# Layer 0 of a four-layer network: the first stage of the state-space scan moved up, its output products put at one tile

## The chip, the cores and the metric

The kernel runs on one core of a Trainium2 chip. A core has a matrix engine (PE, with its weight loads listed as PEld), a vector engine (DVE), an activation engine (ACT), a general engine (POOL) and a sequencer that only issues transfers here (SP); each takes its own instructions in program order and waits for the others through semaphores. The metric is device time in microseconds (us), the median of the runs; a profile is taken of one execution of its own.

## The reference, cut to what matters

The network has four layers on an image batch of 4 x 96 x 64 x 64. Only layer 0 is touched. It is two Mamba blocks (`NLAYERS` = 2) over sequences of 4096 positions, followed by a small fusion and a batch norm:

```
h  = layernorm(seq);  xs, z = split(h @ in_w)
xc = silu(sum_k conv_w[:, k] * shift(xs, k) + conv_b)
dt, Bm, Cm = split(xc @ xproj_w)
delta = softplus(dt @ dt_w + dt_b)
state[t] = exp(delta * A) * state[t-1] + delta * Bm * xc     # 192 channels x 16 states
y = sum over states(state * Cm) + Dp * xc
seq = seq + (y * silu(z)) @ out_w
```

Layers 1 to 3 (a convolution block, attention and feed-forward, a Fourier block) follow after it.

## The kernel before, in words

**Items and tiles.** The sequence is cut into 4 pieces of 1024 positions. With 4 batches and 2 blocks this gives 32 *items* (`items`; index k; the block i alternates every four items). An item's 192 x 16 recurrences are 24 *tiles* of 128 lanes x 1024 positions, in the list `order`. Each tile is one DVE scan (`scan`, L595). Four of them per third use a product `u` that DVE makes first (L586), two take it from POOL (`up`, L571, group GP), two straight from PE (`uta`, group GA). The decay `da`/`dap` is one exponential on ACT (`exp`, L560). After a pair of tiles POOL multiplies the states by C (`times_c`, L600) and PE sums them over the states into a bank y (`sum_y`, L617). `start_y` (L610) puts Dp * xc into that bank first, and `gate` (L628) multiplies y by silu(z). State tiles `hs` are four buffers, given out by `keeps`: a scan that takes one anew has to wait for the `sum_y` of the group that had it before.

**One program order, written by hand.** The loop near the end of `layer0` runs over m, one step per tile, and writes for each step what every engine issues: the scan, the fill of a PE bank for a coming tile (`fills`), the exponential three tiles ahead (one ahead for GP), `times_b`, `times_c`, then `start_y`, `sum_y`, `gate` by the tables `starts`, `sums`, `gates` (tile number counted from the item's own first tile, so 29 is tile 5 of the next item), the output product `project` and `project_z` with `finish` (L647 to L661), and last the steps of the *first stage* of coming items. PE, DVE, ACT and POOL keep this order exactly (`manual_schedule`). SP isn't in that list: the framework places its transfers itself.

**The first stage.** `first_stage(k)` makes all that item k needs before its scans: normalization, convolution `xc` in three parts (PE L232, copied by ACT L356), silu (L367), the product with `xproj` (L246), its copy `dbl` (L386), `delta` in three parts, softplus (L394), a write of delta to memory (`dd`), the product `du` = delta * xc on POOL (L424) and its write (`ud`, both L413), z, and a transposed, weighted copy `uta` (turned by PE L433, taken back by ACT L438 *into delta's own buffer*, weighted by `weigh`, L451). `at_slot(t)` puts a step at step m = 24k - 24 + t: slots 0 to 23 run beside the scans of item k-1, negative ones beside item k-2, slots from 24 beside item k itself. Below, "tile t" is the tile of the running item at which a step stands: slot -2 is tile 22, slot 27 is tile 3.

**Buffers that matter.** PE's results of the first stage and of the output go through two PSUM tiles in turn (`tile_ps`). `x` has two buffers: one is loaded for the normalization of the next-but-one item (slot -20), one for the residual at the output (`load_x`, L275, at 29 in the main loop). `delta` has one buffer.

Of the kernel before, what the change touches and what calls it, by code (L numbers as in the profile page):

```python
# [50 lines left out]
class Net:  # L51
# [43 lines left out]
    def layer0(self, dram, scratch):  # L95
        tc, nc, ins = self.tc, self.nc, self.ins
        x_in = ins["x"]
        with ExitStack() as ctx:
# [23 lines left out]
            w_x = cp.tile([C + 1, 2, 4, DIN], F32, name="w_x")  # L122
# [3 lines left out]
            dtw = cp.tile([97 + DTR, 2, DIN], F32, name="dtw")  # L126
# [9 lines left out]
            n = cp.tile([C + 1, T + 3], F32, name="n")  # L136
# [11 lines left out]
            GP, GA = 2, 3  # L148
# [78 lines left out]
            def spread(ws, rhs, p):  # L227

                ps = tile_ps(128)
                for k, (w, shift) in enumerate(ws):  # L230
                    for at, rows in both:
                        nc.tensor.matmul(  # L232
                            ps[rows],
                            w[:, 64 * p : 64 * p + 64],
                            rhs[:, at.start + shift : at.stop + shift],
                            start=k == 0,
                            stop=k == len(ws) - 1,
                            skip_group_check=True,
                        )
                return ps  # L240
# [37 lines left out]
            def first_stage(k):  # L278

                b, s, i = items[k]  # L280
                m = made[k]
                steps = {}

                def at_slot(t):
                    def keep(f):
                        steps.setdefault(t - 24, []).append(f)

                    return keep
# [61 lines left out]
                def parts_of(name, ws, rhs, slots, bufs):  # L350


                    def into(p, ps):
                        if p == 0:
                            m[name] = early.tile([128, 3, MB], F32, name=name, tag=name, bufs=bufs)
                        nc.scalar.copy(m[name][:, p], ps)  # L356

                    for p, (t, out) in enumerate(slots):
                        at_slot(t)(lambda p=p: m.update({(name, p): spread(ws, rhs, p)}))
                        at_slot(out)(lambda p=p: into(p, m[name, p]))  # L360


                parts_of("xc", [(w_x[:, i, k], k) for k in range(4)], n, ((-6, -4), (-3, -2), (0, 0)), 2)

                @at_slot(1)
                def _():
                    nc.scalar.activation(m["xc"], m["xc"], AF.Silu)  # L367
                    if k:
                        silu_z(k - 1)
                    exp_set()  # L370
# [4 lines left out]
                nb = 6 * NST + DTR  # L375
                dbl = m["dbl"] = dbls[k % 2]

                @at_slot(3)
                def _():
                    m["ps"] = [tile_ps(128), tile_ps(128)]  # L380
                    join([ps[:nb] for ps in m["ps"]], xproj[:, :, i], m["xc"])

                @at_slot(4)
                def _():
                    for at, ps in zip(halves, m["ps"]):
                        nc.scalar.copy(dbl[:nb, at], ps[:nb])  # L386
                    cd = m["cd"] = dram.tile([2 * NST, T], F32, name="cd", tag="cd", bufs=2)
                    nc.sync.dma_start(cd, dbl[: 2 * NST])

                parts_of("delta", [(dtw[:, i], 0)], dbl, ((5, 5), (6, 6), (7, 7)), 1)  # L390

                @at_slot(7)
                def _():
                    nc.scalar.activation(m["delta"], m["delta"], AF.Softplus)  # L394
                    exp_set()

                @at_slot(8)
                def _():
                    m["tb"] = y_bank(3 * k - 2)[:, : 8 * 2 * NST].rearrange("p (q s) -> p q s", q=8)
                    for q in range(8):  # L400
                        nc.tensor.transpose(
                            m["tb"][:, q], dbl[: 2 * NST, q * 128 : q * 128 + 128], self.ident[: 2 * NST, : 2 * NST]
                        )

                @at_slot(9)
                def _():
                    m["bt"] = cp.tile([128, 8, 4], F32, name="bt", tag="bt", bufs=2)
                    nc.scalar.copy(m["bt"], m["tb"][:, :, 4 * GA : 4 * GA + 4])
# [3 lines left out]
                    for at, rows in both:  # L412
                        nc.sync.dma_start(to.rearrange("(p c) t -> c p t", p=3)[:, :, at], m[name][rows])  # L413

                @at_slot(8)
                def _():
                    spread_out("delta", "dd")

                @at_slot(10)
                def _():  # L420
                    m["du"] = m["delta"]
                    if k == 0:
                        m["du"] = early.tile([128, 3, MB], F32, name="z", tag="z", bufs=2)
                    (nc.gpsimd if k else nc.vector).tensor_mul(m["du"], m["delta"], m["xc"])  # L424
                    spread_out("du", "ud")
# [29 lines left out]
                        )  # L455

                e = 0
                for t, count in ((19, 4), (20, 5), (21, 5), (22, 4), (23, 6), (24, 6), (28, 2)):
                    at_slot(t)(lambda of=range(e, e + count): weigh(of))
                    e += count  # L460

# [44 lines left out]
            items = [(b, s, i) for s in range(NSC) for i in range(2) for b in range(B)]  # L506
# [14 lines left out]
            keeps = {(0, 0): 0, (0, GP): 1, (0, 1): 2, (0, GA): 3, (1, 0): 0, (1, GP): 1, (1, GA): 2, (1, 1): 3}  # L521
            keeps |= {(2, GA): 0, (2, 0): 3, (2, GP): 1, (2, 1): 2}
            ends = {max(t for t, x in enumerate(order) if x[:2] == (p, g)): (p, g) for p in range(3) for g in range(4)}
            sums = {4: (0, 0), 8: (0, 1), 9: (0, GP), 11: (0, GA), 13: (1, 0), 17: (1, 1), 18: (1, GP), 19: (1, GA)}
            sums |= {21: (2, GA), 22: (2, 0), 25: (2, 1), 27: (2, GP)}
            starts = {4: 0, 12: 1, 18: 2}
            gates = {13: 0, 21: 1, 29: 2}
            NTL = len(order)
            last = len(items) * NTL
# [100 lines left out]
            def project(k):  # L630
                b, s, i = items[k]
                pss = made[k]["out"] = [tile_ps(), tile_ps()]
                for at, ps in zip(halves, pss):
                    w = fus[:, 0] if i else self.ident[:C, :C]
                    nc.tensor.matmul(ps, w, made[k]["x"][:, at], start=True, stop=False)

            def project_z(k):
                b, s, i = items[k]
                join(made[k]["out"], fo if i else out_w, made[k]["z"], start=False)
# [35 lines left out]
            with tc.manual_schedule(engines=engines):  # L675
                gp = global_pool()
                first = min(stages[0])
                for m in range(first, last + 19):
                    k, t = divmod(m, NTL)
                    if 0 <= m < last:  # L680
                        scan(m)
                    if m == -12:
                        fill(0)
                    if t in fills and 0 < 24 * k + fills[t] < last and m >= 0:
                        fill(24 * k + fills[t])
                    if 0 <= m + 1 < last and on_pool(m + 1):
                        exp(m + 1)
                    if 0 <= m + AHEAD < last and not on_pool(m + AHEAD):
                        exp(m + AHEAD)
                    if t in b_slots:  # L690
                        ahead, p, j = b_slots[t]
                        if 0 <= k + ahead < len(items):
                            times_b(k + ahead, p, j)
                    for back, f in ((1, times_c), (3, keep_state)):
                        k0, t0 = divmod(m - back, NTL)
                        if 0 <= k0 < len(items) and t0 in ends:
                            f(k0, *ends[t0])
                    for k0 in range(max(k - 1, 0), min(k + 1, len(items))):
                        at = m - NTL * k0
                        if at in starts:  # L700
                            start_y(k0, starts[at])
                        if at in sums:
                            sum_y(k0, *sums[at])
                        if at in gates:
                            gate(k0, gates[at])
                        if at == 29:
                            made[k0]["x"] = load_x(*items[k0])
                        if at == 32:
                            project(k0)
                        if at == 33:  # L710
                            project_z(k0)
                        if at == 34:
                            finish(k0)
                    for k0 in range(max(k - 1, 0), min(k + 3, len(items))):
                        for f in stages[k0].get(m - NTL * k0, ()):
                            f()
                    if m in (10, 11):
                        next(gp)
# [877 lines left out]
```

## Time and profile before

| | |
|---|---|
| median of 3 runs | 3871.77 us (3863.05 to 3873.45) |
| the profiled execution | 3861.26 us, its span 3859.4 us |
| first scan starts | 69.1 us |
| last scan of layer 0 ends | 2553.2 us |
| busy from 100 to 2500 us: DVE | 2191.23 us of 2400 |
| the same: POOL | 2077.30 us |
| the same: PE | 1980.54 us, mean granted clock 0.89 |
| the same: ACT | 1904.46 us |
| a DVE scan (L595, with state and rep) | 2337 ns |
| a POOL product with C (L600) | 4180 ns |
| an ACT exponential (L560) | 1149 ns |

A busy time is the sum over an engine's instructions. A wait is named by the engine that waits and by what released it. Layer 0 takes the span's first two thirds; an item takes 71.8 to 85.2 us from its first scan to the next item's, the very first one 87.9.

### The profile page before, as it was taken

What the parts mean: (1) busy time and instruction counts of PE and PEld (TensorE: products, weight loads), DVE (VectorE), ACT (ScalarE), POOL (GpSimd) and SP (SyncE); (2) the same over time, 40 slices, a digit from 0 to 9 for tenths busy, and PEclk for the clock granted to TensorE, in tenths of its full rate; (3) what the DMA queues carried; (4) which work ended last, traced back from release to release, by engine and by line L of the source; (5) the groups of instructions that cost most, each with busy time, mean ns of one, the idle gap of its engine ahead of it and who ended that gap; (6) DMA issues with size and microseconds to landing.
All of it is one profiled execution on the core that took longest, in us unless ns stands there. A gap on an engine that the chain in (4) does not pass through costs nothing. (4 is left out here: it accounts for less than half of the span.)

```text
span 3859.4 us, 46789 instructions
## 1 busy us (share of the span) xinstructions
PE 3226.2 (84%) x15326; PEld 1468.0 (38%) x15326; DVE 2989.2 (77%) x2644; ACT 2722.0 (71%) x5456; POOL 2566.3 (66%) x922
## 2 busy tenths in 40 slices
PE   7788888888888888888788888756899998999988
PEld 3232333323332333232322232226544534666643
DVE  5898888899989898998899999962473384444649
ACT  6787877888778787887788787741245686656557
POOL 1898888888888888988888998941001064534527
PEclk8898888899888898998898998757899999999999
DMA  7566555566656565665655766546200000011101
GB/s 189 146 152 163 144 150 148 148 157 160 160 142 157 137 156 145 166 153 143 155 150 145 170 156 167 142 121 209 98 1 1 1 1 6 17 34 34 39 9 58
DMA packets 171643, 446.62 MB, mean 116 GB/s; under 512 B 48756, under 2 KB 50750, under 8 KB 168064
## 3 DMA queue, kind: packets, MB, share of 16 engines
q1 hardware_dynamic: 171400, 443.64, 44.7%
q8 instruction: 121, 1.98, 0.2%
q14 instruction: 122, 1.00, 0.1%
HBM read 369.97 MB, written 73.50 MB: 115 GB/s over the span
## 5 line engine op out<-in xcount | busy, mean ns | idle before, releaser
L600 POOL TENSOR_TENSOR hs<-hs,crep 128x2048 f32<-128x2048 f32 x384 | 1597.3, 4180 | 333.2 <-DVE hs L595 248.2
L560 ACT ACTIVATE da<-ddb,nega 128x1024 f32<-128x1024 f32 x576 | 661.3, 1149 | 157.4 <-DVE hs L595 138.3
L595 DVE TENSOR_TENSOR_SCAN hs<-da,state,rep 128x1024 f32<-128x1024 f32 x288 | 667.9, 2337 | 46.8 <-PE rep L544 35.2
L571 POOL TENSOR_TENSOR up<-udb,brep 128x1024 f32<-128x1024 f32 x192 | 452.7, 2358 | 74.9 <-DMA udb<-ud 60.5
L617 PE MATMUL y<-hs,sel_r 128*32 128x512 f32 x3072 | 441.9, 650 | 25.5 <-POOL hs L600 25.5
L232 PE MATMUL ps<-n,w_x 97*64 97x512 f32 x1536 | 425.9, 699 | 0.0
L549 PE MATMUL rep<-dbl,sel_b 32*128 32x512 f32 x768 | 250.7, 730 | 175.7 <-DVE hs L595 174.6
L451 ACT ACTIVATE uta<-delta,bt 128x192 f32<-128x192 f32 x1024 | 375.3, 442 | 0.0
L595 DVE TENSOR_TENSOR_SCAN hs<-dap,state,up 128x1024 f32<-128x1024 f32 x144 | 336.3, 2335 | 39.4 <-PE y L617 16.9
L595 DVE TENSOR_TENSOR_SCAN hs<-da,state,u 128x1024 f32<-128x1024 f32 x144 | 338.1, 2348 | 21.7 <-PE y L617 6.8
L544 PE MATMUL rep<-ident,uta 128*128 128x128 f32 x1536 | 224.4, 293 | 74.4 <-DVE hs L595 73.8
L586 DVE TENSOR_TENSOR u<-udb,rep 128x1024 f32<-128x1024 f32 x192 | 236.0, 1229 | 64.1 <-PE rep L549 26.3
L560 ACT ACTIVATE dap<-ddb,nega 128x1024 f32<-128x1024 f32 x192 | 213.9, 1114 | 86.7 <-DVE hs L595 86.1
L544 PEld LDWEIGHTS rep<-ident,uta 128*128 128x128 f32 x1536 | 182.1, 150 | 169.0 <-DVE hs L595 89.2
L232 PEld LDWEIGHTS ps<-n,w_x 97*64 97x64 f32 x1536 | 133.8, 158 | 289.7 <-issue 251.2
L1154 POOL CAST hq<-y 128x1536 fp8e5<-128x1536 f16 x64 | 93.9, 1466 | 217.6 <-issue 122.6
L595 DVE TENSOR_TENSOR_SCAN hs<-da,rep 128x1024 f32<-128x1024 f32 x96 | 216.9, 2277 | 20.1 <-PE rep L544 16.7
L586 DVE TENSOR_TENSOR rep<-udb,rep 128x1024 f32<-128x1024 f32 x192 | 232.3, 1210 | 0.0
L617 PEld LDWEIGHTS y<-hs,sel_r 128*32 128x32 f32 x3072 | 62.3, 111 | 360.9 <-issue 233.9
L549 PEld LDWEIGHTS rep<-dbl,sel_b 32*128 32x128 f32 x768 | 65.1, 201 | 301.8 <-issue 164.1
L246 PE MATMUL ps<-xc,xproj 64*102 64x512 f32 x384 | 129.3, 824 | 58.0 <-ACT xc L367 58.0
L1293 POOL TENSOR_TENSOR av<-av,ec 128x780 f32<-128x780 f32 x32 | 58.7, 1836 | 133.5 <-ACT av L1290 133.5
(275 smaller groups left out, 6290.9 us busy)
## 6 DMA issues: line engine op xcount, KB each, us to landing
ddb<-dd SPq DMA_DIRECT2D x768, 128.0 KB
udb<-ud SPq DMA_DIRECT2D x768, 128.0 KB
crep<-cd SPq DMA_DIRECT2D x512, 128.0 KB
dd<-delta SPq DMA_DIRECT2D x64, 384.0 KB
band<-in_band SPq DMA_DIRECT2D x24, 1024.0 KB
ud<-delta SPq DMA_DIRECT2D x62, 384.0 KB
brep<-cd SPq DMA_DIRECT2D x128, 128.0 KB
x<-in_x SPq DMA_DIRECT2D x32, 384.0 KB
```

The source lines that it names most:

```text
L232: nc.tensor.matmul(ps[rows], w[:, 64 * p : 64 * p + 64], rhs[:, at.start + shift : at.stop + shift], start=k == 0, stop=k == len(ws) - 1, ...
L246: nc.tensor.matmul(ps, w[rows, p], x[rows, p], start=start and p == 0, stop=p == 2)
L451: nc.scalar.mul(m["uta"][:, q, :, 32 * s4 : 32 * s4 + 32].rearrange("t (p j) d -> t p j d", p=3), m["udt"][:, :, q].rearrange("t p (j d) - ...
L544: nc.tensor.transpose(x[:, q * 128 : q * 128 + 128], made[k]["uta"][:, q, 2 * h + j], self.ident)
L549: nc.tensor.matmul(x[:, at], sel_b[rows, g], made[k]["dbl"][rows, at], start=True, stop=True)
L560: nc.scalar.activation(da, made[k]["dd", h, j], AF.Exp, scale=nega[:, col : col + 1])
L571: nc.gpsimd.tensor_mul(up, made[k]["ud", p][:, j], made[k]["brep", GP])
L586: nc.vector.tensor_mul(u, made[k]["ud", h][:, j], x)
L595: nc.vector.tensor_tensor_scan(hs[:, 1:], made[k].pop(("da", t)), u, st, ALU.mult, ALU.add)
L600: nc.gpsimd.tensor_mul(hs[:, :, :T], hs[:, :, 1:], twice(made[k]["crep", g]))
L617: nc.tensor.matmul(made[k]["y", p][row : row + 32], sel_r, made[k]["hs", p, g][:, j, at], start=False, stop=True, skip_group_check=True,)
L1154: nc.gpsimd.tensor_copy(q, y2, saturate=False)
```

## The change: what it does

It leaves every operation as it is and moves steps in the hand-written order.

- Convolution: part 3 goes from slot 0 to slots -2 (PE) and -1 (copy). Silu, with silu of the previous item's z and the reload of the exponential table, goes from slot 1 to -1.
- `xproj` from 3 to 1, the copy `dbl` from 4 to 2; delta's parts from 5, 6, 7 to 3, 3, 5 (PE) and 5, 5, 6 (copy); softplus from 7 to 6.
- The transposed B from 8 and 9 to 6 and 7, the write of delta from 8 to 7, `du` and its write from 10 to 8.
- `weigh`: twelve of its 32 instructions go from tiles 23 and 0 (six each) to tiles 0, 1, 2, 3 (three each).
- Sums into y: (0,1) from 8 to 7, (1,0) from 13 to 14, (2,1) from 25 to 26. The term Dp * xc of the first third from tile 4 to tile 0.
- Output: the residual's load from 29 to 27; `project` stays at 32 (tile 8), `project_z` joins it there from 33, `finish` goes from 34 to 33. These three now stand in a loop of their own after the sums and gates.

```diff
-                parts_of("xc", [(w_x[:, i, k], k) for k in range(4)], n, ((-6, -4), (-3, -2), (0, 0)), 2)
-                @at_slot(1)
+                parts_of("xc", [(w_x[:, i, k], k) for k in range(4)], n, ((-6, -4), (-3, -2), (-2, -1)), 2)
+                @at_slot(-1)
                 def _():
                     nc.scalar.activation(m["xc"], m["xc"], AF.Silu)
...
-                @at_slot(3)
+                @at_slot(1)
                     join([ps[:nb] for ps in m["ps"]], xproj[:, :, i], m["xc"])
-                @at_slot(4)
+                @at_slot(2)
                         nc.scalar.copy(dbl[:nb, at], ps[:nb])
-                parts_of("delta", [(dtw[:, i], 0)], dbl, ((5, 5), (6, 6), (7, 7)), 1)
-                @at_slot(7)
+                parts_of("delta", [(dtw[:, i], 0)], dbl, ((3, 5), (3, 5), (5, 6)), 1)
+                @at_slot(6)
                     nc.scalar.activation(m["delta"], m["delta"], AF.Softplus)
-                @at_slot(8)
+                @at_slot(6)
                     m["tb"] = y_bank(3 * k - 2)[:, : 8 * 2 * NST].rearrange("p (q s) -> p q s", q=8)
-                @at_slot(9)
+                @at_slot(7)
                     m["bt"] = cp.tile([128, 8, 4], F32, name="bt", tag="bt", bufs=2)
-                @at_slot(8)
+                @at_slot(7)
                     spread_out("delta", "dd")
-                @at_slot(10)
+                @at_slot(8)
                     m["du"] = m["delta"]
...
-                for t, count in ((19, 4), (20, 5), (21, 5), (22, 4), (23, 6), (24, 6), (28, 2)):
+                for t, count in ((19, 4), (20, 5), (21, 5), (22, 4), (24, 3), (25, 3), (26, 3), (27, 3), (28, 2)):
...
-            sums = {4: (0, 0), 8: (0, 1), 9: (0, GP), 11: (0, GA), 13: (1, 0), 17: (1, 1), 18: (1, GP), 19: (1, GA)}
-            sums |= {21: (2, GA), 22: (2, 0), 25: (2, 1), 27: (2, GP)}
-            starts = {4: 0, 12: 1, 18: 2}
+            sums = {4: (0, 0), 7: (0, 1), 9: (0, GP), 11: (0, GA), 14: (1, 0), 17: (1, 1), 18: (1, GP), 19: (1, GA)}
+            sums |= {21: (2, GA), 22: (2, 0), 26: (2, 1), 27: (2, GP)}
+            starts = {0: 0, 12: 1, 18: 2}
...
-                        if at == 29:
+                    for k0 in range(max(k - 1, 0), min(k + 1, len(items))):
+                        at = m - NTL * k0
+                        if at == 27:
                             made[k0]["x"] = load_x(*items[k0])
                         if at == 32:
                             project(k0)
+                            project_z(k0)
                         if at == 33:
-                            project_z(k0)
-                        if at == 34:
                             finish(k0)
```

## The prediction

> **What bounds the kernel now.** I read first how busy the engines are in layer 0, then who DVE waits for, then the places in time where those waits stand. Busy times of three items, 1, 8 and 12 (columns: stretch, its length, then busy us of PE, PEld, DVE, ACT, POOL, granted PE clock, DMA share, GB/s):
>
> ```profile
> 157.00:228.80 71.80, 59.27 (x320) 22.64 (x318) 69.61 (x39) 61.24 (x123) 67.15 (x20) 0.98 0.57 144
> 703.60:782.80 79.20, 62.86 (x320) 23.53 (x318) 71.17 (x40) 63.23 (x129) 67.24 (x20) 0.91 0.58 148
> 1004.80:1084.30 79.50, 67.45 (x320) 24.85 (x318) 71.20 (x40) 61.59 (x123) 67.16 (x20) 0.86 0.61 149
> ```
>
> DVE has some 70 to 71 us of work in every item; the items differ in what it waits. Item 1 shows that 71.8 us can be had, 8 and 12 lose about 8 each. So the floor is DVE's work, and a reordering can win DVE's waits and nothing else. From 160 to 2550 us DVE waits for (us in total, times, longest):
>
> ```profile
> DVE hs L595 <- PE rep L544: 46.1, 14, 4.7
> DVE hs L595 <- PE y L617: 28.2, 26, 4.9
> DVE hs L595 <- ACT x L647: 26.2, 4, 6.9
> DVE u L586 <- PE rep L549: 22.3, 18, 2.1
> DVE u L586 <- DMA udb<-ud: 9.7, 6, 1.9
> DVE hs L595 <- ACT dap L560: 9.7, 19, 1.4
> DVE hs L595 <- ACT shift L655: 6.5, 1, 6.5
> ```
>
> These are 148.7 us. In time they fall into two places. *Tiles 17 to 21 of 13 items*: the rows L544, L586 <- L549 and udb, 46.1 + 22.3 + 9.7 = 78.1, and about ten of the 28.2 (0.8 a time at tile 18): 88 us. *Tile 10*: ACT x and shift, 32.7, and the rest of L617, 18: 51 us, of which items 3, 4, 5, 12, 18 and 21 have 5 to 7 each. L560 is tile 2.
>
> The first place, item 8, in order of time (start, duration, instruction; brackets: idle before and releaser), SP, then POOL, ACT, DVE:
>
> ```profile
> 737.65 0.31 SPq L661 DMA_DIRECT2D scratch<-x  x1
> 746.41 0.33 SPq L275 DMA_DIRECT2D x<-in_x  x1
> 746.84 1.24 SPq L413 DMA_DIRECT2D ud<-delta  x2
> ```
> ```profile
> 738.28 3.45 POOL L424 TENSOR_TENSOR delta<-delta,xc 128x1536 f32<-128x1536 f32 x1
> ```
> ```profile
> 752.99 0.58 ACT L438 COPY delta<-y 128x512 f32<-128x512 f32 x1 [5.75 <-DMA ud<-delta]
> ```
> ```profile
> 756.56 2.35 DVE L595 TENSOR_TENSOR_SCAN hs<-da,state,rep 128x1024 f32<-128x1024 f32 x1 [3.23 <-PE rep L544]
> 760.74 1.23 DVE L586 TENSOR_TENSOR u<-udb,rep 128x1024 f32<-128x1024 f32 x1 [1.84 <-DMA udb<-ud]
> ```
>
> POOL has du at 741.73. Its write stands on SP behind a load of x, which itself stands behind the write of the output and waits until PE has read the x buffer (L299, tile 13): it leaves at 746.84, five us late. ACT may not overwrite delta before the write has read it, so L438 holds ACT for 5.75 us, behind it PE's turns and fills, and tile 17 comes late. The waits of SP count this (same columns as above):
>
> ```profile
> SPq L275 <- PE ps L299: 116.8, 13, 10.9
> ```
>
> Thirteen times, in the 13 items.
>
> The second place, item 12, on PE and then DVE:
>
> ```profile
> 1029.56 3.70 PE L635 MATMUL ps<-x,ident 96*96 96x512 f32 x4 [1.43 <-DMA x<-in_x]
> 1033.19 1.94 PE L617 MATMUL y<-hs,sel_r 128*32 128x512 f32 x8
> 1036.05 4.51 PE L246 MATMUL ps<-z,out_w 64*96 64x512 f32 x12
> 1040.48 1.06 PE L617 MATMUL y<-hs,sel_r 128*32 128x512 f32 x8
> ```
> ```profile
> 1041.72 2.35 DVE L595 TENSOR_TENSOR_SCAN hs<-dap,state,up 128x1024 f32<-128x1024 f32 x1 [6.16 <-ACT x L647]
> ```
>
> The products wait 1.43 us for x, then run at half clock (in item 9 the same three groups take 1.96, 1.06 and 2.82), and behind them stands the sum (0,GP) whose state buffer scan 10 needs. L647 is only the last ACT instruction before: the sum, ending at 1041.54, is what released it.
>
> [...] part 2 of the convolution, behind steady work, takes 3.65 us, part 3, behind an idle 2.85 us and a fill, 5.84 (item 12). But 1.43 us of idle time was enough at 1029.56[...]
>
> **The change part by part.**
>
> *SP's order and du (tile 8).* In the changed program both loads of x follow `cd` directly, with PE's reads of them an item old, and `ud` follows one `ddb` load; the output's write comes after `ud`. POOL's du goes ahead of one `up` (2.35) and one product with C (4.18): in item 12 it would start where the group (0,GA) ends, 1033.9, instead of 1040.3, 6.4 us earlier. Softplus's end (1031.5 there) allows it. SP is then free, so `ud` leaves 9 to 11 us earlier in the 13 items, lands with the measured 6.2 us (746.84 to 752.99) well before tile 14, and L438 doesn't wait. What du delays on POOL, `up` of (1,1) and the product (1,0) by 3.45 us, is wanted at tiles 14 and 16; at 1044 it has caught up. Sum (1,0) at tile 14 for 13 fits. Removed: 88, of which I take 80 as small waits stay.
>
> *Output at tile 8.* x is loaded after `dbl`, which is some 5 us earlier (below), so the 1.43 us go. `project` and `project_z` together, 1.96 + 2.82, now follow sum (0,1); a delta part (1.08) and the transposes of B (0.68) leave the row. From the fill of tile 8 to the end of sum (0,GP) PE needs 1.13 + 1.06 + 1.96 + 2.82 + 1.06 = 8.0 us, against 9.4 in item 9 (803.96 to 813.33), at full clock. DVE needs two scans and two products from there, and has them: tile 10 falls to some 0.3 us a time, 51 to 10. Removed: 40.
>
> *Silu at tile 23.* This is what costs. PE puts part 3 straight behind the last sum of tile 22 (ends 1077.98 before item 13), 3.65 at full clock: 1081.6. On ACT follow the copy, 0.56, table, silu, silu, table (1.28 + 1.48 + 1.47 + 1.28 = 5.5, as in the trace at 1091.49 to 1096.94), an exponential (1.05 to the next start), three `weigh` (0.35 each): 1089.8. `dap` then lets scan 2 go 1.2 later, 1091.0, where without a wait it would go at 1090.2. So 0.8 us at tile 2, 1.3 in items whose sum ends 0.4 later, in place of 0.3 on average (9.7 / 30): + 0.7 x 30 = 20. The fill of tile 0, now behind part 3, ends at 1082.8 and is wanted at 1083.0: no cost at full clock, and if late it takes the place of the tile 2 wait. Twelve `weigh` (4.2 us) in tiles 0 to 3 fill what silu left there; the last ones at tile 4 end as before, within 0.3 us. `xproj` can start when silu ends (1084.9), and with two exponentials and six `weigh` between, `dbl` is copied at about 1094.5, not 1101.
>
> *Rest.* Dp * xc at tile 0 needs a bank whose gate was tile 21: nothing. Sums (0,1), (2,1): POOL's products end 1025.6 and at 1085, one tile ahead: nothing. delta's parts, tables, counts of instructions and bytes: the same. `finish` one tile earlier: about -2 at the end.
>
> *PE's pauses.* New ones: before the fill of tile 3 (about 2 us), before delta (2), before the first uta fill (2.4). A half-clocked fill, delta part, fill (1.1 each) before scan 7 would cost about 1 us, and some in tile 8. From below nothing; from above 2 us an item. I take 0.4 x 31 = 12.
>
> Sum: -80 - 40 + 20 + 12 - 2 = -90, 3861.3 to 3771. The profiled execution is 10.5 us under the median of the three; I put the median between the two, 3780.
>
> **The rivals.**
> - *Only the queue is mended.* The tile-10 wait stays, since the pauses leave PE at half clock in front of two products: -80 + 20 + 12 - 2, about 3811, up to 3840 with twice the tile 2 cost. For: 5 to 7 us came from a pause of only 1.43. Against: x isn't late any more.
> - *No change* (3860 to 3883): both gains real, and 3 us an item lost again (92 / 31), where ACT's row at tile 23 is held by a late part 3. Against: PE ran part 2, just ahead, at 3.65 us, without a pause between.
> - *Slower.* PE is at half clock from tile 5 to 10 in every item, not in six. The pass from the fill of tile 8 to the sum took 15.6 us in item 12 for 9.4 in item 9: 6.2 x 31 = 192 on top of the sum, 3780 + 192 = 3970. It decides from 3.3 us an item on (103 us from 3780 to 3883, over 31 items). For: three pauses of 2 us ahead of that stretch. [...]
>
> **How the numbers follow.** A median of three spread by 0.3% (3863 to 3873) tells no less than that: 12 us. Both waits gone 0.62 (own range 3745 to 3815), only the queue 0.18, no change 0.06, slower 0.14. Faster 0.62 + 0.18 = 0.80. The range leaves out slower and no change, 0.20: upper end 3860. Lower end: 88 and 51 all gone and no new cost at tile 2 or by pauses, 3861 - 141 = 3720, which I think hardly possible as tile 2's chain is serial; 3740.
>
> **What would show it.** No row of SP's x load waiting for L299 and no L438 wait on `ud` above 2 us; DVE waits for L544 under 10 us in all. At tile 2 a wait of 0.8 to 1.3 us for `dap` in nearly every item: if it is 3 or more, part 3 ran at half clock. At tile 10 no wait over 2 us. POOL's du before the `up` of tile 9. Items of 73 to 75 us each. Wrong I am if waits at tiles 7, 8 or 10 return in most items, or if POOL, at 67 of 73 us, becomes what DVE waits for.

## The result, and the profile after

The changed kernel takes **3873.12 us** (median of 20 runs, 3866.59 to 3899.71), the kernel before 3867.98 (20 runs beside them, 3845.14 to 3886.94): a ratio of **1.0028**, 95% interval 1.0010 to 1.0047. That is no change, or slower by less than half a percent; it lies in the range that the prediction called no change (3860 to 3883), and 93 us above the forecast 3780. The profiled execution of after has a span of 3885.5 us, 26 more than before's 3859.4. That is more than the 5 us between the medians, because the profiled execution of after is 14 us above its median and that of before 7 below.

The table is DVE's idle time in layer 0 between one scan and the next, by tile, worked out from the traces (us per item, mean of 32 items; the sum is over all tiles of layer 0). DVE idles 0.1 to 0.3 us at some tiles in every kernel, as at tile 12 before; tiles that never have more are left out.

| kernel | tile 2 | 7 | 10 | 12 | 15 | 16 | 17 | 18 | 21 | sum |
|---|---|---|---|---|---|---|---|---|---|---|
| before | 0.52 | 0.00 | 1.66 | 0.27 | 0.08 | 0.00 | 1.54 | 1.14 | 0.59 | 219 |
| after | 1.30 | 0.25 | 0.50 | 0.54 | 0.28 | 0.64 | 0.00 | 1.73 | 1.15 | 244 |

The wait at tile 17 is gone, that at tile 10 mostly; tiles 2, 7, 12, 15, 16, 18 and 21 have taken more than both gave. Items 5 and 12 of after (stretch, length, busy us of PE, PEld, DVE, ACT, POOL, granted PE clock, DMA share, GB/s):

```profile
469.98:548.42 78.44, 64.80 (x318) 23.45 (x318) 69.84 (x40) 63.40 (x131) 67.11 (x20) 0.89 0.60 151
1019.57:1094.04 74.47, 59.18 (x318) 23.23 (x318) 71.16 (x39) 61.49 (x123) 67.11 (x20) 0.98 0.59 151
```

Before, most items were good (72 to 75) or bad (79 to 85). Now, of the 31 items between two first scans, 20 take 78.4 to 79.4 and five 74.5 to 74.8; DVE's own work is as it was. What DVE waits for most from 160 to 2550 us (total, times, longest):

```profile
DVE u L586 <- PE rep L549: 69.6, 59, 2.2
DVE hs L595 <- PE rep L544: 35.4, 54, 1.6
DVE hs L595 <- ACT dap L560: 23.5, 23, 1.1
DVE hs L595 <- PE y L617: 22.5, 27, 3.3
```

Fills (L549) were 22.3 us in 18 waits; they are 69.6 in 59. SP has no row any more for a load of x that waits for L299. Where the forecast gain went shows in item 5, on PE, then POOL, DVE and ACT. L299 is `center`, the first product of a coming item's normalization; a *turn* is one of the three steps in which PE transposes du (L433):

```profile
501.04 1.06 PE L544 MATMUL rep<-ident,uta 128*128 128x128 f32 x8 [1.77 <-DVE hs L595]
503.13 2.08 PE L549 MATMUL rep<-dbl,sel_b 32*128 32x512 f32 x4 [1.03 <-DVE hs L595]
...
511.80 1.13 PE L299 MATMUL ps<-center,x 96*128 96x96 f32 x8
514.21 1.13 PE L299 MATMUL ps<-center,x 96*128 96x96 f32 x8 [1.28 <-ACT z L356]
...
516.14 1.07 PE L617 MATMUL y<-hs,sel_r 128*32 128x512 f32 x8
517.14 0.66 PE L433 MATMUL y<-ident,delta 128*128 128x128 f32 x4
...
522.46 0.90 PE L433 MATMUL y<-ident,delta 128*128 128x128 f32 x4 [2.41 <-ACT delta L438]
523.29 2.08 PE L549 MATMUL rep<-dbl,sel_b 32*128 32x512 f32 x4
```
```profile
501.57 3.43 POOL L424 TENSOR_TENSOR delta<-delta,xc 128x1536 f32<-128x1536 f32 x1 [2.31 <-DMA dd<-delta]
```
```profile
525.41 1.23 DVE L586 TENSOR_TENSOR u<-udb,rep 128x1024 f32<-128x1024 f32 x1 [2.15 <-PE rep L549]
527.47 2.29 DVE L595 TENSOR_TENSOR_SCAN hs<-da,u 128x1024 f32<-128x1024 f32 x1 [0.82 <-PE y L617]
```
```profile
511.49 1.12 ACT L560 ACTIVATE dap<-ddb,nega 128x1024 f32<-128x1024 f32 x1
512.54 1.14 ACT L560 ACTIVATE da<-ddb,nega 128x1024 f32<-128x1024 f32 x1
513.58 0.57 ACT L356 COPY z<-ps 128x512 f32<-128x512 f32 x1
```

Three things are to be seen. First, PE pauses 1.77 and 1.03 us at tiles 9 to 11, as its fills are ahead of DVE, and the next fill runs at half clock (2.08 for 1.13). Second, the L617 at 516.14 is sum (1,0), which the change put at tile 14: it stands between the last fill and du's first turn (L433), and PE pauses 1.28 us ahead of it for ACT's third copy of z, which has two exponentials in front. Third, what comes behind is one serial chain: turn, ACT's copy L438 with ACT's other work, last turn (522.46), fill of tile 18 (to 525.37), and DVE waits at 18. Over the items, the last turn starts a median of 21.7 us after scan 10 starts, in the kernel before 18.8.

### The profile page after: what moved, and what is told of

The parts are those of the page before. It is cut to its first block, busy times and chain, and to the rows that moved or that the text cites. A ratio compares the mean times of both kernels' runs of the same rounds, so it can differ in the third digit from the quotient of the medians.

```text
span 3885.5 us, 46905 instructions
## 1 busy us (share of the span) xinstructions
PE 3203.9 (82%) x15326; PEld 1468.9 (38%) x15326; DVE 2991.4 (77%) x2644; ACT 2716.7 (70%) x5456; POOL 2565.6 (66%) x922
## 3 DMA queue, kind: packets, MB, share of 16 engines
q14 instruction: 123, 1.01, 0.1%
## 5 line engine op out<-in xcount | busy, mean ns | idle before, releaser
L617 PE MATMUL y<-hs,sel_r 128*32 128x512 f32 x3072 | 469.3, 696 | 15.9 <-POOL hs L600 15.8
L549 PE MATMUL rep<-dbl,sel_b 32*128 32x512 f32 x768 | 254.1, 735 | 128.9 <-DVE hs L595 128.9
L232 PE MATMUL ps<-n,w_x 97*64 97x512 f32 x1536 | 355.4, 601 | 0.0
L544 PEld LDWEIGHTS rep<-ident,uta 128*128 128x128 f32 x1536 | 193.2, 156 | 236.6 <-issue 163.2
L232 PEld LDWEIGHTS ps<-n,w_x 97*64 97x64 f32 x1536 | 108.8, 137 | 240.1 <-issue 185.9
L617 PEld LDWEIGHTS y<-hs,sel_r 128*32 128x32 f32 x3072 | 67.5, 115 | 341.5 <-issue 226.4
L232 PE MATMUL ps<-dbl,dtw 103*64 103x512 f32 x384 | 138.0, 742 | 66.1 <-ACT dbl L386 50.8
L424 POOL TENSOR_TENSOR delta<-delta,xc 128x1536 f32<-128x1536 f32 x31 | 106.4, 3432 | 74.0 <-DMA dd<-delta 63.8
L549 PEld LDWEIGHTS rep<-dbl,sel_b 32*128 32x128 f32 x768 | 67.1, 205 | 226.1 <-issue 150.7
```

The costliest lines, as they stand in the source:

```text
L232: nc.tensor.matmul(ps[rows], w[:, 64 * p : 64 * p + 64], rhs[:, at.start + shift : at.stop + shift], start=k == 0, stop=k == len(ws) - 1, ...
L544: nc.tensor.transpose(x[:, q * 128 : q * 128 + 128], made[k]["uta"][:, q, 2 * h + j], self.ident)
L549: nc.tensor.matmul(x[:, at], sel_b[rows, g], made[k]["dbl"][rows, at], start=True, stop=True)
L617: nc.tensor.matmul(made[k]["y", p][row : row + 32], sel_r, made[k]["hs", p, g][:, j, at], start=False, stop=True, skip_group_check=True,)
```

## The experiments

**x off SP.** In before, the bad items had a load of x on SP ahead of du's write. *q1* issues the loads of x from ACT:

```diff
-                nc.sync.dma_start(x, xd[:, b] if i else ...)
+                nc.scalar.dma_start(x, xd[:, b] if i else ...)
```

> The kernel before with one edit: both loads of x are issued from ACT's queue, in ACT's written order, so no load of x stands on SP ahead of the write of du. Theory Q (the SP queue holds the write of du in 13 items, worth about 80 us): the waits of L438 on ud and of DVE on L544 at tile 17 go, time about 3868 - 80 = 3790. Rival R (mending the queue only uncovers another late chain of the same length on PE, as the changed kernel suggests): 3840 to 3870.

4004.83 us, ratio 1.0361 (1.0323 to 1.0398): both missed. The wait at tile 17 is gone from every item (1.54 to 0.00, with 18 at 0.63), but tile 10 waits 8.15 us an item instead of 1.66: SP's next loads of delta and u (L492) now wait for transfers of x, up to 17 us at a time, and the loads of C stand behind them on SP.

```profile
SPq L492 <- DMA x<-xd: 290.8, 29, 17.4
```
```profile
POOL hs L600 <- DMA crep<-cd: 296.1, 25, 13.2
```

POOL's products wait for C, the sums for POOL, and scan 10 for a sum. So the total tells nothing of the queue. Tile 17 agrees with theory Q, but not cleanly: L438 still waits for `ud` 29 times, though never above 3.2 us (before, 14 waits up to 7.1), and scans that start 8 us later at tile 10 may hide some of it.

*q2* instead loads the residual x two tiles earlier, in a loop of its own as in after; SP then has that load ahead of du's write in all items:

```diff
-                        if at == 29:
+                        if at == 27:     # in a loop over k0 behind the sums and gates
                             made[k0]["x"] = load_x(*items[k0])
```

> The kernel before with one edit: the residual's load of x at 27 in a loop of its own, as in the change. In the built program this puts a load of x that waits for PE directly ahead of the write of du in every item, not in 13. Theory Q: 17 more items with 6.5 us, less some 35 us at tile 10 as x comes earlier: 3868 + 110 - 35 = 3943. Rival R: within 20 us of 3868.

3907.76 us, ratio 1.0119 (1.0077 to 1.0160). SP's wait for L299 comes 29 times (251.9 us), not 13, and tile 17 waits 3.28 us a time for 1.54, but tile 10 falls to 0.22: slower by half of what was expected (38 us for 75), with the mechanism as expected. The queue was a real cost, and after has none of it.

**What took its place: POOL (P), or PE's half clock (H)?** POOL waits in after, ahead of du, for the write of delta:

```profile
POOL delta L424 <- DMA dd<-delta: 61.7, 26, 2.7
```

*p1* puts du and its write at tile 9, *z1* gives PE three products with zeros in its pause; they add zero to y, which keeps its values, and take 1.0 us each.

```diff
-                @at_slot(8)
+                @at_slot(9)
                 def _():
                     m["du"] = m["delta"]
```

> The changed kernel with du and its write at slot 9, behind the POOL product up of that tile, in place of slot 8. POOL then has work while delta's write is still reading. Rival P (POOL's 2.1 us wait for delta's write before du sets the time): 30 x 2.1, 3873 - 60 = 3813. Theory H: within 15 us of 3873.

```diff
+            none = cp.tile([128, 128], F32, name="none")     # memset to 0
+            def add_zero(k):
+                nc.tensor.matmul(made[k]["y", 0], none, made[k]["xc"][:, 0], start=False, stop=True, ...)
...
+                        for _ in range({9: 2, 10: 1}.get(at, 0)):
+                            add_zero(k0)
```

> The changed kernel with three extra PE products of 128x512 by an all-zero matrix, added into the bank of y (two behind the sum of tile 9, one at tile 10), which leave the sums as they are and fill PE's pause there. Theory H (the pause at tiles 9 to 11 brings PE to half clock at tiles 10 to 12, and that lateness is what DVE pays at tiles 12 to 21): the slow stretch 32 to 39 us after an item's start goes, items fall from 78.5 to about 75 us, time 3873 - 85 = 3790. Rival P (POOL is late, as du waits for delta's write): no gain, 3873 to 3885.

p1 3869.29 us, 0.9997 (0.9978 to 1.0016); z1 3871.56, 1.0018 (0.9998 to 1.0038). Against after's 3873 neither is worth anything, so neither P nor H is the whole cause. z1 does what it should at tiles 12 and 15 (0.54 to 0.25, 0.28 to 0.04), but 16, 18 and 21 stay at 0.54, 1.71 and 1.15, and the windows of 3.41 us that PE spends at half clock in items 1 to 30 stay as many (132 of 683, in after 135 of 688): something else holds the chain.

**Sum (1,0).** *s1* is p1 with sum (1,0) back at tile 13; *b1* is before with nothing but this sum at 14.

```diff
-            sums = {..., 11: (0, GA), 14: (1, 0), 17: (1, 1), ...}
+            sums = {..., 11: (0, GA), 13: (1, 0), 17: (1, 1), ...}      # s1; b1 the reverse
```

> The kernel after with du at tile 9 (as in p1, 3869) and besides sum (1,0) back at tile 13, where the kernel before has it. Theory S: at tile 14 this sum stands on PE directly ahead of du's first turn and takes the 1.1 us of slack that the chain turn, copy, squares, fill of tile 18 had (turn 14.1 us after scan 10 in the best items, 13.0 before). Then the waits at tiles 15 to 21 leave most of the 22 items that have them, about 4 us each: 3869 - 88 = some 3780. Rival C (PE's pauses and the half clock behind them, whatever the order of the sums): no change, 3869 within 15.

> The kernel before with sum (1,0) at tile 14 instead of 13, nothing else. Theory S: the 17 items without the wait of the queue lose their slack of 1 us at tiles 18 and 21 and then 2 to 3 us each: +35 to +50, some 3910. Rival C: within 12 us of before, 3868.

s1 3813.83 us, 0.9863 (0.9847 to 0.9879); b1 3902.31, 1.0113 (1.0073 to 1.0152). One entry of a table costs the kernel before 34 us (28 to 59 by the interval) and, taken back, gives the changed one some 55 (to p1). The traces say how. Half way through `center` PE has to wait for ACT to copy z's third part away, since both go through the same two PSUM tiles, and ACT comes to that copy only behind two exponentials (item 5 above). At tile 13 the sum stands ahead of z's third part and runs in time that PE would wait anyway. With the sum at 14 PE waits that time idle, and the sum is paid behind it, ahead of the turn. PE's wait for that copy in before, after and b1, in this order:

```profile
PE ps L299 <- ACT z L356: 15.6, 29, 0.6
```
```profile
PE ps L299 <- ACT z L356: 42.4, 29, 1.7
```
```profile
PE ps L299 <- ACT z L356: 47.4, 29, 1.7
```

From scan 10 to du's first turn, the shortest of 29 items is 12.8 us in before (median 13.0) and 13.0 in s1 (14.8), but 14.1 in after (16.4) and 13.9 in b1 (15.7). The medians hold the half clock behind PE's pauses as well (item 5 of after: 2.08 us for a fill of 1.13). In s1, item 4, with no pause at `center`:

```profile
416.17 2.02 PE L299 MATMUL ps<-center,x 96*128 96x96 f32 x16
418.03 1.04 PE L544 MATMUL rep<-ident,uta 128*128 128x128 f32 x8
418.90 0.60 PE L433 MATMUL y<-ident,delta 128*128 128x128 f32 x4
...
424.17 0.66 PE L433 MATMUL y<-ident,delta 128*128 128x128 f32 x4 [0.60 <-ACT delta L438]
```

Tile 16 falls from 0.69 to 0.00 there, 18 from 1.49 to 0.48. s1 won less than the 88 us expected (4 us in 22 items): tiles 12, 15, 18 and 21 still wait 0.47, 0.31, 0.48 and 0.50, and tile 10 is back at 0.67, for 0.10 in p1.

**Both together.** *s3* is s1 with z1's three products.

> Kernel s1 with three products with a matrix of zeros on PE (two at tile 9, one at 10, 128 x 512 each, added to y's first half, so that y keeps its values). If S and C both hold, the two together leave only the wait at tile 2 in most items: 3755 to 3775. S alone: as s1, within 12. C alone: as the kernel with zeros alone, 3871 within 12.

3768.32 us, 0.9747 (0.9724 to 0.9769), within the range expected. The zeros that gave nothing in after give 46 us here: tiles 12, 15, 16, 18 and 21 are at 0.24, 0.00, 0.00, 0.22 and 0.21, and du's first turn comes at 13.0 us in the median item. The windows at half clock fall from 121 of 665 in s1 to 75 of 654, so the gain goes with the clock. Two causes held one chain: with the sum at 14 the pauses didn't matter (z1), with it at 13 and du at 9 they do. 55 and 46 us together are a little more than the 93 that the forecast missed.

**Why the sum can't simply go back.** *s2* is after with the sum at 13 and du left at tile 8; *s4* the same with the three products.

> The kernel after with sum (1,0) back at tile 13 alone, du left at tile 8. If du at tile 8 keeps POOL's product (1,0) back, as it ends 41.5 us into an item there, PE waits 1.5 to 2.2 us for it at tile 13, falls to half clock, and nothing is won: 3855 to 3885. If POOL doesn't matter and only the sum's place ahead of du's first turn does: as s1, 3814 within 12.

> The kernel after with sum (1,0) at tile 13 and the three products with zeros, du left at tile 8; s3 without its first edit. If du at tile 8 is what forbids the sum at tile 13: 3830 to 3870. If not: as s3, 3768 within 12.

s2 3855.05 us, 0.9955 (0.9933 to 0.9977), at the lower edge of what the first theory gave: 18 us under after, not the 59 of s1; s4 3895.37, 1.0069 (1.0044 to 1.0094), beyond its upper end. PE and POOL of s4, item 4 (its lines are two higher):

```profile
422.20 3.44 POOL L426 TENSOR_TENSOR delta<-delta,xc 128x1536 f32<-128x1536 f32 x1 [2.25 <-DMA dd<-delta]
...
427.92 4.18 POOL L602 TENSOR_TENSOR hs<-hs,crep 128x2048 f32<-128x2048 f32 x1
```
```profile
432.15 1.33 PE L619 MATMUL y<-hs,sel_r 128*32 128x512 f32 x8 [3.29 <-POOL hs L602]
433.41 1.98 PE L234 MATMUL ps<-n,w_z 97*64 97x512 f32 x4
435.32 3.73 PE L301 MATMUL ps<-center,x 96*128 96x96 f32 x16
```

du at tile 8, with POOL's wait of 2.25 us ahead of it, pushes POOL's product (1,0) to 432.1; the sum waits for it for 3.29 us, z and `center` behind run at half clock (3.73 for 2.02 in s1), and tile 15 waits 3.15 us an item. It is POOL's wait that counts, not du's place: du, one `up` and product (1,0) end 12.2 us after the POOL product ahead of them here, and 9.8 in s1, item 4, where `up` stands first and no wait is left. The sum waits for POOL 0.08 us an item in s1, 0.98 in s2 and 2.35 in s4: the earlier PE is, the longer it waits, so the zeros make it worse here. p1 had du at 9 for nothing only because its sum was still at 14.

**Is it the change or the zeros?** *b3* is before with the three products; *o1* is after with its output put back to before's tiles, in before's loop.

```diff
-                        if at == 27:
+                        if at == 29:
                             made[k0]["x"] = load_x(*items[k0])
                         if at == 32:
                             project(k0)
-                            project_z(k0)
                         if at == 33:
+                            project_z(k0)
+                        if at == 34:
                             finish(k0)
```

> The kernel before with the three products with zeros at tiles 9, 9 and 10. Its PE has the products of the output there and no pause to fill. If the zeros are worth something only where the change left a pause: 3868 within 12. If they lift PE's clock in any order of the work: 30 to 50 less, some 3825.

> The kernel after with the output alone put back (load of x at 29, the two products at tiles 8 and 9, the last step at 10). SP's order around the writes of delta and du stays that of the kernel after. If the output at tile 8 is what shortens tile 10, as the prediction had it (40 us): some 3910. If tile 10 is short because x comes earlier behind cd, and the pause of PE at tiles 9 to 11 is filled by the products: 3850 to 3870, with tiles 12 and 15 below 0.1 us a time instead of 0.54 and 0.28.

b3 3861.10 us, 0.9994 (0.9973 to 1.0016): the zeros alone do nothing for before. o1 3866.73, 1.0000 (0.9983 to 1.0018): tile 10 is at 0.10 with the output back, so it isn't short because both products stand at tile 8. It is short because x is there: in before's items 3, 4, 5, 12, 18 and 21 the loads of x, right behind `cd`, leave 18.4 to 19.8 us into the item, in o1 and after some 12, as the first stage moved up. q2, where only the residual's load comes earlier, has 0.22 there. My side expectation for tiles 12 and 15 missed (0.52 and 0.30, not below 0.1): PE's order at the products is the same in both, as nothing stands between tiles 8 and 9 on PE, and so is its pause at tiles 9 to 11.

**A version that beats both.** *s5* adds four products with zeros to s3, in PE's pauses ahead of the fill of tile 3 and of the first `uta` fill:

```diff
-                        for _ in range({9: 2, 10: 1}.get(at, 0)):
+                        for _ in range({2: 2, 5: 2, 9: 2, 10: 1}.get(at, 0)):
```

> Kernel s3 with four more products with zeros, two at tile 2 and two at tile 5, in PE's pauses ahead of the fill of tile 3 (2.5 us) and of the first fill by transposes (2.7 us). If the half clock behind these pauses makes the wait of 1 to 4 us at tile 10 in six items (15 us in all) and part of that at tile 7: 3745 to 3760. If the products themselves come in the way of the parts of delta: 3768 or above.

**3749.79 us**, 0.9688 (0.9664 to 0.9712). Tile 10 falls from 0.48 to 0.00, items take 73.0 to 74.4, and the sum of the idle time is 102 us. 36 of 648 windows are at half clock. What is left is tile 2 and the first item; the largest of DVE's waits in s5 from 160 to 2430 us:

```profile
DVE hs L597 <- ACT dap L562: 18.9, 25, 1.2
```

The other kernels in the form of the first table:

| kernel | tile 2 | 7 | 10 | 12 | 15 | 16 | 17 | 18 | 21 | sum | us |
|---|---|---|---|---|---|---|---|---|---|---|---|
| q1 | 0.41 | 0.00 | 8.15 | 0.27 | 0.04 | 0.00 | 0.00 | 0.63 | 0.64 | 359 | 4005 |
| q2 | 0.35 | 0.00 | 0.22 | 0.27 | 0.04 | 0.00 | 3.28 | 1.94 | 0.98 | 260 | 3908 |
| b1 | 0.34 | 0.00 | 0.99 | 0.27 | 0.05 | 0.54 | 0.88 | 2.07 | 1.01 | 230 | 3902 |
| b3 | 0.40 | 0.03 | 1.48 | 0.26 | 0.00 | 0.00 | 1.57 | 1.14 | 0.67 | 221 | 3861 |
| p1 | 1.27 | 0.19 | 0.10 | 0.53 | 0.32 | 0.69 | 0.00 | 1.49 | 1.04 | 219 | 3869 |
| o1 | 1.26 | 0.20 | 0.10 | 0.52 | 0.30 | 0.68 | 0.00 | 1.45 | 1.03 | 216 | 3867 |
| z1 | 1.31 | 0.15 | 0.64 | 0.25 | 0.04 | 0.54 | 0.00 | 1.71 | 1.15 | 227 | 3872 |
| s2 | 1.24 | 0.23 | 0.62 | 0.43 | 1.51 | 0.06 | 0.00 | 0.55 | 0.72 | 212 | 3855 |
| s4 | 1.24 | 0.22 | 0.41 | 0.24 | 3.15 | 0.05 | 0.00 | 0.53 | 0.60 | 249 | 3895 |
| s1 | 1.23 | 0.19 | 0.67 | 0.47 | 0.31 | 0.00 | 0.00 | 0.48 | 0.50 | 164 | 3814 |
| s3 | 1.09 | 0.20 | 0.48 | 0.24 | 0.00 | 0.00 | 0.00 | 0.22 | 0.21 | 120 | 3768 |
| s5 | 1.10 | 0.22 | 0.00 | 0.25 | 0.00 | 0.00 | 0.00 | 0.22 | 0.21 | 102 | 3750 |

A row is of one execution: b1's has a span of 3876.3, below its median of 3902, so its sum shows less than the 34 us.

## Why the prediction was wrong

- **SP's order, "Removed: 88, of which I take 80".** The mechanism was right: the block on SP and the wait of L438 for `ud` are gone, tile 17 is at 0.00 (49 us of the sum), and q1 and q2 move it both ways. The step that failed is the next sentence: "Sum (1,0) at tile 14 for 13 fits". It puts the move at nothing; it looks at whether the sum's input is ready, not at what stands behind the sum on PE. Behind it stands du's turn, and from there the chain that ends at tile 18. Tiles 15, 16, 18 and 21 went from 1.81 to 3.80 us an item, 64 us of the sum. s1 against p1 puts 55 us on this one entry, b1 shows it in the kernel before.
- **"Softplus's end (1031.5 there) allows it".** It doesn't: du overwrites delta in place, and so waits until `dd` has read it. So du starts 31.8 us into an item for 35.2 before (medians of 30), 3.4 earlier for the forecast 6.4. POOL's idle time ahead of L424 for that is 61.7 us in after (26 times, longest 2.7), against 4.0 before (7 times). The waits of before name that releaser too; the prediction took du's start from POOL's queue and softplus alone. By itself it costs nothing (p1), but it is what keeps product (1,0) from being ready at tile 13 (s2, s4): with du at 8 the sum can't stand at 13 without a wait.
- **"PE's pauses ... I take 0.4 x 31 = 12".** Mis-sized. Of the three pauses that it names, two were filled in s5, ahead of the fill of tile 3 and of the first `uta` fill: 18.5 us, near the 12. What it lacks are the pauses at tiles 9 to 11 (1.77 and 1.03 us in item 5), worth 46 us once the sum is back (s3), and at `center` (1.28).
- **Output at tile 8, "51 to 10. Removed: 40".** The size was right (1.66 to 0.50 us, 37), and so was its first reason, that x comes earlier with `dbl` (10.2 us into an item for 16.9). The second, both products in one place, gave nothing: o1 has tile 10 at 0.10 with the output left where it was.
- **Silu at tile 23, + 20.** Right: tile 2 went from 0.52 to 1.30, 25 us in 32 items, and the longest wait for `dap` is 1.1 for the forecast 0.8 to 1.3.
- **The rivals.** "No change" named the right result for a wrong reason (3 us an item lost at tile 23). "Slower", whose 0.14 was my estimate, had the right kind, half clock behind PE's pauses in most items (135 of 688 windows in all), but at tiles 5 to 10, where little is lost. None named the chain from du's turn to the fill of tile 18. Nor did the signs of being wrong: the waits came at tiles 15 to 21, not in most items at 7, 8 or 10, nor from POOL.

The first table checks the rest: between the two profiled executions DVE's idle time rose by 25 us and the span by 26.

## What to carry to other kernels

When a step moves past another in an engine's written order, ask what stands behind it in its new place and which pause it filled in its old one: here one sum of 1.06 us filled a pause for free at one slot and cost 34 to 55 us in all at the next. Before a stall's removal is booked as a gain, find the next chain that ends at the same wait and its slack: here the 1.1 us from 13.0 to 14.1 used it up. When one edit alone gives nothing, as with p1 and z1, test it together with the other suspects: both were needed once the sum was back.

## What the runs showed of the hardware

- Short pauses were enough for the half clock. The granted clock in the traces of before and after changes only in steps of 3.413 us (the windows), between full and half. In items 1 to 30 of after none of the 84 windows that were followed by a fall was idle throughout: PE had been busy for 0.15 to 0.66 of them (median 0.42). All 470 windows that were followed by full clock again had 0.43 or more. In item 5, 1.77 us of pause and the first 0.15 of the next, in the window up to 502.25, were followed by two windows at half clock, and 15 of the 32 items have such two, 32 to 39 us after their start. So in after a window that was partly idle was enough. Between 0.43 and 0.66 both happened: there the busy share alone does not tell which clock follows.
- Some items fall in step with the windows. Items 1 to 7 of after take 78.4 to 78.7 us, 23 windows of 3.413 us (78.5), each with the half clock 32 to 39 us after its start; in s3 items 15 to 22 repeat every four items, 300.4 us for 88 windows (300.3). So a pattern that cost time came again in seven items in a row. That the step with the window is the cause was not tested.
- More work on PE made the kernel faster: three products with zeros an item (3 us of PE's time) took 46 us off s1, seven took 64, with a mean granted clock over the span of 0.909, 0.932 and 0.951 in s1, s3 and s5; the same three took nothing off before and after (3861.10 and 3871.56 us).
